# Three layers of scans and attention on one core: softplus's sum on TensorE, late folds for GpSimd's products, and a shorter lag in the last attention

## The chip, the cores and the metric

One core of a Trainium2 chip runs the kernel. The metric is the device time of one execution in microseconds, lower being better; the figure for a kernel is the median of its runs.

## The reference

Four conditioned layers in a row over a batch of B = 2, T = 1024 positions, D = 256 channels, all in float32. Layers 0 and 1 are state-space layers (inner width 512, 16 states per channel; layer 1 has one scan forwards and one backwards), layers 2 and 3 are attention with 16 heads of width 16. Cut to what matters here:

```python
# layer 0; layer 1 does the same twice (z1, and z2 on flipped time)
dt = softplus(dt_r @ dt_proj_w.T + dt_proj_b)          # (b, s, 512)
def step(h, inp):                                      # over s = 1024
    dA = exp(dt_t[:, :, None] * A)                     # A = -exp(A_log)
    h = h * dA + (dt_t * u_t)[:, :, None] * B_t[:, None, :]
    y = einsum('bdn,bn->bd', h, C_t)
y = (ys + u * D_param) * silu(z)

# layer 2: softmax of q over its 16 channels, of masked k over positions
attn = einsum('bhse,bhsd->bhed', k, v)

# layer 3
att = einsum('bnhl,bmhl->bnmh', q, k) + (1 - mask) * -1e6
att = softmax(att, axis=2)
y = einsum('bnmh,bmhl->bnhl', att, v)
h = layer_norm(y) * (1 + scale) + shift
return x + silu(h) @ out_w + out_b
```

## The kernel before

**Scans.** Six scans run one after the other: layer 0 for both batches, then layer 1 forwards and backwards for each batch. A scan has 512 channels x 16 states. A tile is 32 channels x 4 states on the 128 partitions and all 1024 positions on the free axis, so a scan has 64 tiles, and `chain` (L985) goes through them in 192 pairs for all six. One tile needs:

- `decay` (L922): ScalarE makes exp(dt * A) into a PSUM tile `dA` (two of them);
- `inputs` (L928): GpSimd multiplies the spread dt*u with B into an SBUF tile `hb` (eight of them), L930;
- `tile` (L933): VectorE runs the recurrence in one instruction (L941, or L937 backwards), then the product with C is made on VectorE (L944) or, where `far` is set, on GpSimd (L943). `far` is set for the first tile of a pair only, by a counter (`lead`) that adds up how much more VectorE has than GpSimd and takes in the background work that GpSimd was given;
- `fold` (L962): TensorE sums the four states of each channel with a 128x32 matrix into a PSUM bank `ys`, two halves of 512 for each tile. Both tiles of a pair are folded in the next pair, after its first slot of background work.

**Background.** While the scans run, everything else (projections, normalisations, softplus, the attention of the first batch in layer 2, its projections in layer 3) is a queue of Python generators in `Behind` (L798). Twice in each pair `slot` (L832) runs some of their steps: it is given a credit of matmul columns (`RATES`, one for each scan, the credit capped at 2T) and stops where the credit or the budgets for ScalarE and GpSimd are used up. A step ends at a `yield`. `pipe` (L366) starts up to two matmul groups, in two PSUM banks, before it empties the first. The order of instructions on each engine is the order of these calls; nothing reorders it later.

**Softplus** is made in `ssm_inputs` (L550) for each of four blocks of 128 channels: `high` projects dt, `parts` takes |x| and max(x, 0) on ScalarE, ScalarE makes ln(1 + exp(-|x|)), `both` (L602) adds the two on GpSimd (`far_op`, L137, issued at L139) and multiplies with u, also on GpSimd.

**Attention, the tail.** After the last scan the second batch still has layers 2 and 3 to pass, as background work, while `attention` (L1360) already runs layer 3 for the first batch. The heads lie in groups of four; each head has 32 rows of a query and a key tile, of which 16 are the head, one carries a constant and one the row's maximum or the mask. For each of 8 groups (two batches of four) there are 16 steps of maxima (TensorE scores, L1380; VectorE maxima, L1389) and 16 of exponentials (scores again; ScalarE exp; TensorE sums over values, L1420). Maxima run one group, 16 steps, ahead of the exponentials, so the loop has 9 x 16 = 144 steps, the first 16 with maxima alone and the last 16 with exponentials alone. In every step two background slots are run, of one generator step each. PSUM in this stage: six banks `sc` for scores, one `av` for the sums, one `bank` for background work. `layer3` (L1279) projects queries and keys with weights padded to 32 columns a head, so that a group is a full 128 rows.

Of the kernel before, what the change touches and what calls it, by code (L numbers as in the profile page):

```python
# [10 lines left out]
F32 = mybir.dt.float32  # L11
# [19 lines left out]
RATES = (2048, 2048, 1250, 1300, 1500, 1500)  # L31
# [4 lines left out]
for _name, _n in (  # L36
# [6 lines left out]
    ("mask3", 16),  # L43
# [9 lines left out]
def kernel(ctx: ExitStack, tc: tile.TileContext, a: dict, out: bass.AP):  # L53
# [23 lines left out]
    banks = {"bank": 2, "ys": 2, "av": 1, "sc": 6}  # L77
# [106 lines left out]
    def row(name):  # L184

        t = small.tile([P, D], F32, tag="row", name="row", bufs=1)
        nc.sync.dma_start(t, a["rows"][0, ts(_ROWS[name], D)].partition_broadcast(P))
        return t
# [207 lines left out]
    def root(mv):  # L396

        r = small_t((P, mv.shape[1]), "rstd", 4)
        act_f(r, mv[:, :, 1], AF.Ln, bias=eps)
        act_f(r, r, AF.Exp, scale=-0.5)  # L400
        return r

    def refine(mv, r):

        q = small_t((P, mv.shape[1]), "newt", 4)
# [17 lines left out]
    def scaled(src, r, q):  # L423
        o = abuf((P, 4, D))
        for j in range(4):
# [61 lines left out]
    def projected(w, src, func, bias, res, keep=True, to=None, count=None):  # L487
# [18 lines left out]
        def ended(m, ch, ps):  # L506
            take(m, ch, ps)
            held[0] -= 1
            if ch == 1:
                if func is AF.Silu:  # L510
                    yield
# [38 lines left out]
    def ssm_inputs(key, u, w_xp, w_dt, dt_b, st):  # L550
# [58 lines left out]

        two = banks["bank"] == 2  # L610
        pss = [high(0, ch) for ch in range(1 + two)]
        yield
        for d in range(4):
# [9 lines left out]
            if d < 3:  # L623
                pss = [high(d + 1, ch) for ch in range(1 + two)]
            yield
            both(d, dt, dt, dtu, ALU.add)
# [8 lines left out]
    def layer0(b, st):  # L635
# [43 lines left out]
        for m in range(4 if b else 0):  # L679
# [24 lines left out]
            yield  # L704
# [10 lines left out]
    def layer1(b, st1, st2):  # L715
# [16 lines left out]
        def first():  # L732
# [5 lines left out]
            for v in skip:  # L738
                nc.vector.tensor_tensor(v, v, twice(cond["s1"][b], 4), ALU.mult)
                far_op(v, v, twice(cond["o1"][b], 4), ALU.add)  # L740
                yield
# [56 lines left out]
    class Behind:  # L798
# [3 lines left out]
        def __init__(self):  # L802
            self.queue = []
            self.soon = []
            self.credit = 0

# [10 lines left out]
        def step(self):  # L817

            while self.queue or self.soon:
# [5 lines left out]
                try:  # L825
                    least = next(self.queue[0])
                    return max(work[0] - at, least or mode["least"])
# [4 lines left out]
        def slot(self, columns):  # L832
# [7 lines left out]
            self.credit = min(self.credit + columns, 2 * T)  # L840
# [3 lines left out]
            while (self.queue or self.soon) and self.credit > 0:  # L844
# [6 lines left out]
                for key in self.room:  # L851
                    self.room[key] -= spent[key]
                    self.given[key] += spent[key]
                    spent[key] = 0

# [14 lines left out]
    class Scan:  # L870
# [91 lines left out]
        def fold(self, d, cp, k, es):  # L962


            for ch in range(2):
                for j, e in enumerate(es):
# [18 lines left out]
    def chain(scans, rates, early, mid, after):  # L985
# [14 lines left out]
        def fold(p):  # L1000
            i, d, cp, k = pairs[p]
            if k == 0:
                scans[i].begin(d, cp)
            scans[i].fold(d, cp, k, [made["inputs"].pop(2 * p + j) for j in range(2)])
# [24 lines left out]
        lead = 0  # L1029
        for p, (i, d, cp, k) in enumerate(pairs):  # L1030
# [17 lines left out]
            behind.slot(rates[i])  # L1048
            if p:
                fold(p - 1)  # L1050
# [29 lines left out]
            behind.slot(rates[i])  # L1080
            s.tile(4 * d + 2 * cp + 1, k, made["decay"].pop(2 * p + 1), made["inputs"][2 * p + 1])
# [39 lines left out]
    def layer2(b, src, dst):  # L1121
        w_qk, w_vo = [weight("w2", 2, 2 * D, 2 * i * D) for i in range(2)]
        w_k = [w_qk[:, :, D:]]
        mneg_i, mneg = abuf((P, T), I32), abuf()
# [68 lines left out]
        r_bq2 = row("bq2")  # L1193
# [81 lines left out]
        yield from stylize(b, y, "aff2", w_vo[:, :, D:], row("bo2"), src, dst, to=x_of[3][b])  # L1275
# [3 lines left out]
    def layer3(b, st):  # L1279

        xn = []
        w_q, w_k = [[weight("qk_w3", 2, DI, at)] for at in (0, DI)]
# [31 lines left out]

        for g in range(4):
            while b and st["n"] < g:

                yield
            qa, ka = [abuf(pool=act if b else None) for _ in range(2)]

            def put(o, ch, bias, ps):
                act_f(o[:, ts(ch, 512)], ps, AF.Identity, bias=bias)
# [9 lines left out]
            yield  # L1332

# [26 lines left out]
    def attention(sts, done):  # L1360
# [70 lines left out]
        half1 = None  # L1431
        for n in range(-1, len(groups)):
            has_e, has_m = n >= 0, n + 1 < len(groups)
            sts[1]["n"] = n
            half0 = None
            for step in range(2 * NT):
                if half1 is not None:
                    next(half1)
                if step == 9 and has_m:
                    half0 = maxima(n + 1, 0)  # L1440
                if half0 is not None and step < 12:
                    next(half0)
                es = [hb() for _ in range(2)] if has_e else None
                for part in range(2):
                    e = [2 * part, 2 * part + 1]
                    m = [2 - 2 * part, 3 - 2 * part]
                    if not has_m:
                        e, m = (range(4), []) if part == 0 else ([], [])
                    if not has_e:
                        e, m = ([], range(4)) if part == 0 else ([], [])  # L1450
                    made = []
# [239 lines left out]
```

## Time and profile before

| what | value |
|---|---|
| median of three runs | 2152.08 us (2148.35 to 2152.58) |
| the profiled execution | 2153.55 us, span from first to last instruction 2151.8 us |
| TensorE matmul busy | 1702.0 us (79%), granted clock 0.821 on average |
| VectorE busy | 1728.3 us (80%) |
| ScalarE busy | 1165.3 us (54%) |
| GpSimd busy | 1318.0 us (61%) |
| 384 inputs on GpSimd, L930 | 898.5 us, 2368 ns each |
| 384 recurrences on VectorE, L941 and L937 | 877 us, some 2.28 us each |
| 285 products with C on VectorE, L944 | 348.9 us, 1224 ns each |
| 99 products with C on GpSimd, L943 | 234.0 us, 2364 ns each |
| 2048 score records on TensorE, L1380 | 357.8 us |

The times come from a profile of one execution. An engine's busy time is the union of its instructions. A wait is put down to the instruction that released it last. TensorE shows two records for each float32 matmul. The scans run from about 70 to 1475 us, the tail from there to 2152 us.

### The profile page before, as it was taken

Reading aid. Unit: us, or ns where it says so; the run is one execution under the profiler, and the core shown is the slowest. Engines: PE = TensorE matmul, PEld = TensorE weight load, DVE = VectorE, ACT = ScalarE, POOL = GpSimd, SP = SyncE. Lnnn points to the kernel's source line nnn. Section 1 sums busy time; section 2 is a strip of 40 time slices with the busy share of each in tenths; the row PEclk is TensorE's granted clock in tenths of the full one; section 3 lists DMA queues with packets and bytes.
Section 4 is the critical chain, followed back from the end, with each engine's and each line's share of the span. In section 5 each row is a group of like instructions: output and inputs, shape, how many; then the busy total and the mean of one; then the engine's idle time right before and its main releaser. Section 6 shows DMA issues by size and latency. Waiting matters only on the chain.

```text
span 2151.8 us, 22746 instructions
## 1 busy us (share of the span) xinstructions
PE 1702.0 (79%) x8144; PEld 642.7 (30%) x8144; DVE 1728.3 (80%) x1688; ACT 1165.3 (54%) x1631; POOL 1318.0 (61%) x651
## 2 busy tenths in 40 slices
PE   7577876488786747888856778647899999999996
PEld 3132213132231312212313323204344433343333
DVE  4688898898999999999998979996767646777742
ACT  5566675475546446564554445431245555655575
POOL 0799897998899999999997879994001000000000
PEclk9688968598895559959856868856799999999998
DMA  3664367264844545558552253433000100010001
GB/s 110 243 215 134 128 231 257 62 204 157 304 156 148 184 155 176 192 171 293 175 186 101 93 198 107 142 110 118 8 1 23 48 2 2 18 55 1 2 1 37
DMA packets 106117, 265.94 MB, mean 124 GB/s; under 512 B 14123, under 2 KB 38572, under 8 KB 106005
## 3 DMA queue, kind: packets, MB, share of 16 engines
q1 hardware_dynamic: 106004, 264.50, 35.9%
q8 instruction: 64, 1.05, 0.2%
q14 instruction: 49, 0.39, 0.1%
HBM read 196.43 MB, written 67.90 MB: 123 GB/s over the span
## 4 chain that ended last, share of the span: by engine, by line
PE 30%; DVE 14%; POOL 8%; issue 6%; ACT 3%; DMA 1%; SPq 0%; DVEq 0%; ACTq 0%; POOLq 0%
PE sc_t L1380 13%; PE bank_t L93 7%; PE av_t L1420 6%; POOL hb_t L930 5%; DVE dA_t L937 3%; DVE dA_t L941 3%; DVE mh L1389 2%; POOL hb_t L943 2%; ACT act_t L131 2%; PE bank_t L97 1%; PE ys_t L968 1%; DVE hb_t L937 1%; DVE hb_t L944 1%; DVE hb_t L941 1%; ACT dA_t L131 1%
## 5 line engine op out<-in xcount | busy, mean ns | idle before, releaser
L930 POOL TENSOR_TENSOR hb_t<-sp,bc 128x1024 f32<-128x1024 f32 x384 | 898.5, 2368 | 58.1 <-DMA bc<-bc 21.1
L131 ACT ACTIVATE dA_t<-sp,negA 128x1024 f32<-128x1024 f32 x384 | 428.0, 1116 | 526.0 <-DVE hb_t L944 424.4
L968 PE MATMUL ys_t<-hb_t,fold 128*32 128x512 f32 x1536 | 324.6, 799 | 227.2 <-POOL hb_t L943 139.7
L941 DVE TENSOR_TENSOR_SCAN dA_t<-dA_t,hb_t 128x1024 f32<-128x1024 f32 x195 | 445.7, 2286 | 59.6 <-ACT dA_t L131 38.0
L1389 DVE TENSOR_REDUCE mh<-sc_t 128x1 f32<-128x512 f32 x512 | 327.5, 685 | 143.9 <-PE sc_t L1380 143.6
L778 POOL TENSOR_TENSOR act_t<-act_t,row 128x1024 f32<-128x1024 f32 x8 | 18.7, 2350 | 629.2 <-DMA act_t<-x 384.6
L131 ACT ACTIVATE hb_t<-sc_t 128x512 f32<-128x512 f32 x512 | 276.2, 595 | 194.0 <-PE sc_t L1380 193.5
L944 DVE TENSOR_TENSOR hb_t<-dA_t,bc 128x1024 f32<-128x1024 f32 x285 | 348.9, 1224 | 20.9
L1380 PE MATMUL sc_t<-act_t 32*128 32x512 f32 x2048 | 357.8, 660 | 8.6 <-DVE mh L1389 7.4
L943 POOL TENSOR_TENSOR hb_t<-hb_t,bc 128x1024 f32<-128x1024 f32 x99 | 234.0, 2364 | 45.6 <-DVE hb_t L941 39.9
L937 DVE TENSOR_TENSOR_SCAN dA_t<-dA_t,hb_t 128x1024 f32<-128x1024 f32 x90 | 205.6, 2284 | 7.5 <-ACT dA_t L131 4.3
L131 ACT ACTIVATE act_t<-bank_t,cols 128x512 f32<-128x512 f32 (+1 forms) x238 | 151.7, 675 | 89.0 <-PE bank_t L93 73.5
L968 PEld LDWEIGHTS ys_t<-hb_t,fold 128*32 128x32 f32 x1536 | 42.2, 122 | 461.0 <-POOL hb_t L943 193.8
L1420 PE MATMUL av_t<-hb_t,act_t 128*32 128x256 f32 x2048 | 162.5, 391 | 0.4
L1380 PEld LDWEIGHTS sc_t<-act_t 32*128 32x128 f32 x2048 | 124.7, 188 | 125.9 <-issue 72.9
L93 PE MATMUL bank_t<-act_t,w_c_w 128*128 128x512 f32 x256 | 133.1, 671 | 23.6 <-ACT act_t L131 23.6
L941 DVE TENSOR_TENSOR_SCAN hb_t<-dA_t,hb_t 128x1024 f32<-128x1024 f32 x61 | 138.9, 2278 | 0.3 <-ACT dA_t L131 0.3
L139 POOL TENSOR_TENSOR act_t<-act_t 128x1024 f32<-128x1024 f32 x50 | 118.0, 2359 | 2.2 <-ACT act_t L131 1.9
L93 PE MATMUL bank_t<-act_t,w_dt_w 64*128 64x512 f32 x96 | 79.3, 967 | 31.3 <-ACT act_t L131 29.8
L1420 PEld LDWEIGHTS av_t<-hb_t,act_t 128*32 128x32 f32 x2048 | 42.4, 108 | 186.1 <-issue 174.5
L97 PE MATMUL bank_t<-ident,act_t 128*128 128x128 f32 x264 | 61.1, 370 | 42.7 <-ACT act_t L131 40.6
L937 DVE TENSOR_TENSOR_SCAN hb_t<-dA_t,hb_t 128x1024 f32<-128x1024 f32 x38 | 86.6, 2280 | 2.4 <-ACT dA_t L131 2.4
(154 smaller groups left out, 1710.4 us busy)
## 6 DMA issues: line engine op xcount, KB each, us to landing
sp<-dt SPq DMA_DIRECT2D x192, 512.0 KB, 5.7
dt<-act_t SPq DMA_DIRECT2D x48, 512.0 KB, 5.2
bc<-bc SPq DMA_DIRECT2D x48, 512.0 KB, 6.5
u<-act_t SPq DMA_DIRECT2D x24, 512.0 KB, 5.0
fu<-u SPq DMA_DIRECT2D x24, 512.0 KB, 4.0
y<-y SPq DMA_DIRECT2D x96, 128.0 KB, 5.0
g<-act_t SPq DMA_DIRECT2D x16, 512.0 KB, 5.2
fg<-g SPq DMA_DIRECT2D x64, 128.0 KB, 4.2
```

The lines of the kernel that those rows point to most:

```text
L93: nc.tensor.matmul(o, w, x, **kw)
L131: nc.scalar.activation(o, x, func, **kw)
L139: nc.gpsimd.tensor_tensor(o, x, y, op)
L930: nc.gpsimd.tensor_tensor(e, self.sp[c, 1], self.bc[0][k], ALU.mult)
L937: nc.vector.tensor_tensor_scan(h[:, ::-1], dA[:, ::-1], e[:, ::-1], 0.0, ALU.mult, ALU.add)
L941: nc.vector.tensor_tensor_scan(h, dA, e, 0.0, ALU.mult, ALU.add)
L943: return lambda: nc.gpsimd.tensor_tensor(e, h, self.bc[1][k], ALU.mult)
L944: nc.vector.tensor_tensor(e, h, self.bc[1][k], ALU.mult)
L968: nc.tensor.matmul(self.ys[d, cp][at : at + DS, :], fold, e[:, ts(ch, 512)], start=False, stop=(k == NK - 1),)
L1380: nc.tensor.matmul(ps, w[r, ts(at, P)], x[r, ts(wide_at, 512)], start=True, stop=True)
L1389: nc.vector.tensor_reduce(mh[n][:, t, ch, j : j + 1], ps, AX.X, ALU.max)
L1420: nc.tensor.matmul(sums.av[32 * j : 32 * j + 32, ts(part, 256)], sts[b]["v"][t // 2][:, t % 2, 4 * g + j, :], es[j // 2][:, at : at + 256] ...
```

## The change

It has parts in both stages.

In the scans: softplus's sum is made by TensorE (two matmuls with the identity add |.| part and max part into a bank) and copied back by ScalarE, in place of GpSimd's add; the next block's projection is started after it. Where a pair's first product was made on GpSimd, only the second tile is folded at the usual place and the first one after the second slot of the pair. The first two scans give more columns to a slot, the credit's cap is 3T, and a step that yields `ALONE` ends its slot (before each Silu and in layer 1's first normalisation). Layer 2's two bias rows are loaded earlier, with two buffers.

In the tail: the lag between maxima and exponentials is 12 steps (`LAG`), in one loop over 140 steps. Scores and background work share seven `sc` banks. For the second batch, queries and keys are projected unpadded, two blocks of 128 channels, and spread to groups: a memset and an add of the constant rows on GpSimd, then four DMAs a tile. Normalised tiles are scaled on VectorE.

```diff
-RATES = (2048, 2048, 1250, 1300, 1500, 1500)
+ALONE = -1
+RATES = (2600, 2600, 1250, 1300, 1500, 1500)
+LAG = 12
...
-    banks = {"bank": 2, "ys": 2, "av": 1, "sc": 6}
+    banks = {"bank": 2, "ys": 2, "av": 1, "sc": 7}
...
     def scaled(src, r, q):
         o = abuf((P, 4, D))
-        for j in range(4):
+        for j in range(4 if mode["tail"] else 0):
+            nc.vector.tensor_scalar(
+                o[:, j, :], src[:, j, :], r[:, j : j + 1], q[:, j : j + 1], ALU.mult, ALU.add
+            )
+        for j in range(0 if mode["tail"] else 4):
             act_f(
...
+        def summed(x, y):
+            def add(ch):
+                ps = bank()
+                for i, t in enumerate((x, y)):
+                    mm(ps, ident, t[:, ts(ch, 512)], start=(i == 0), stop=(i == 1))
+                return ps
+            yield from pipe(*(
+                (lambda ch=ch: add(ch), lambda ps, ch=ch: act_copy(x[:, ts(ch, 512)], ps))
+                for ch in range(2)
+            ))
...
-            if d < 3:
+            if d < 3 and not (mode["scans"] and two):
                 pss = [high(d + 1, ch) for ch in range(1 + two)]
             yield
-            both(d, dt, dt, dtu, ALU.add)
+            if mode["scans"] and two:
+                yield from summed(dt, dtu)
+                pss = [high(d + 1, ch) for ch in range(2)] if d < 3 else []
+            else:
+                both(d, dt, dt, dtu, ALU.add)
...
-            self.credit = min(self.credit + columns, 2 * T)
+            self.credit = min(self.credit + columns, 3 * T)
...
+                if self.alone:
+                    break
...
             behind.slot(rates[i])
+            split = far
             if p:
-                fold(p - 1)
+                fold(p - 1, (1,) if split else (0, 1))
...
             behind.slot(rates[i])
+            if split:
+                fold(p - 1, (0,))
...
     def layer2(b, src, dst):
+        r_bq2 = row("bq2")
...
-        r_bq2 = row("bq2")
+        r_bo2 = row("bo2")
...
+    def spread_heads(xn, w_qk, mrow, st, put):
+        for c in range(2):
+            flat = []
+            for i, bias in enumerate(("bq3d", "bk3d")):
+                o = abuf()
+                flat.append(o)
+                w = [w_qk[:, :, ts(i, D)]]
+                yield from pipe(*(
+                    (lambda ch=ch: project(w, xn, c, ch),
+                     lambda ps, ch=ch: put(o, ch, col(bias, c), ps)) for ch in range(2)
+                ))
+            for g in (2 * c, 2 * c + 1):
+                while st["n"] < g:
+                    yield
+                both = [abuf(pool=act) for _ in range(2)]
+                for i, t in enumerate(both):
+                    nc.gpsimd.memset(t, 0.0)
+                    nc.gpsimd.tensor_scalar(t, t, col("ones3", i), None, ALU.add)
+                    for j in range(4):
+                        at = 64 * (g % 2) + DH * j
+                        nc.sync.dma_start(t[32 * j : 32 * j + DH, :], flat[i][at : at + DH, :])
+                nc.sync.dma_start(both[1][DH + 1 :: 32, :], mrow)
+                st["qk"].append(both)
+                yield
...
-        for n in range(-1, len(groups)):
-            has_e, has_m = n >= 0, n + 1 < len(groups)
+        going = []
+        steps = 2 * NT * len(groups)
+        for at in range(steps + LAG):
+            has_e, has_m = at >= LAG, at < steps
+            n, step = divmod(at - LAG, 2 * NT)
+            n1, step1 = divmod(at, 2 * NT)
             sts[1]["n"] = n
+            if at % NT == 1 and 0 < at // NT <= 2 * len(groups):
+                going.append(maxima(*divmod(at // NT - 1, 2)))
+            going = [v for v in going if next(v, 0) is None]
...
-    banks["bank"] = 1
-    mode.update(scans=False, tail=True)
+    mode.update(scans=False, tail=True, bank="sc")
```

## The prediction

> **What bounds the kernel now.** I read the tenths first, to find the stages, then the busy time of each stage, then in each stage the waits of the engine that is full.
>
> ```profile
> PE   7577876488786747888856778647899999999996
> DVE  4688898898999999999998979996767646777742
> POOL 0799897998899999999997879994001000000000
> PEclk9688968598895559959856868856799999999998
> ```
>
> Each digit is a slice of 54 us. Up to slice 27 VectorE (DVE) and GpSimd (POOL) are both near full and TensorE (PE) is not: the scans. From slice 28 on GpSimd is empty and TensorE is full at full clock: the last attention. Cut at the turns, the columns being us and then busy us (and instructions) of PE, PEld, DVE, ACT, POOL, the granted clock, the DMA share and GB/s:
>
> ```profile
> 92.00:1474.00 1382.00, 1006.01 (x3270) 351.89 (x3270) 1262.97 (x870) 755.04 (x908) 1267.41 (x610) 0.75 0.50 171
> 1474.00:1560.00 86.00, 74.24 (x260) 39.51 (x255) 55.58 (x104) 14.51 (x25) 5.11 (x3) 0.74 0.18 60
> 1560.00:2105.00 545.00, 536.79 (x4288) 210.93 (x4290) 353.77 (x625) 318.65 (x584) 15.96 (x13) 1.00 0.05 15
> ```
>
> The scans last 1382 us with 1263 on VectorE and 1267 on GpSimd: two bounds of one size, 8% from full. The attention is TensorE's: 537 of 545 us. What the engines wait for within the scans (us in total, times, longest):
>
> ```profile
> PE ys_t L968 <- POOL hb_t L943: 139.7, 36, 8.1
> ...
> ACT act_t L131 <- PE bank_t L93: 55.1, 40, 3.9
> ...
> DVE dA_t L941 <- ACT dA_t L131: 38.0, 22, 4.4
> ...
> DVE act_t L785 <- PE bank_t L93: 19.5, 8, 6.0
> ...
> DVE qmx L1205 <- PE bank_t L93: 8.2, 1, 8.2
> ```
>
> A scan waits for its decay (ScalarE) because ScalarE, in order, sits at an eviction whose matmul stands on TensorE behind a fold that waits for GpSimd's product with C. So a late GpSimd product can reach VectorE over two other engines. Last, one step of the attention without background work:
>
> ```profile
> 2010.47 1.14 PE L1380 MATMUL sc_t<-act_t 32*128 32x512 f32 x8
> 2011.54 0.16 PEld L1420 LDWEIGHTS av_t<-hb_t,act_t 128*32 128x32 f32 x8 [0.76 <-issue]
> 2011.55 0.64 PE L1420 MATMUL av_t<-hb_t,act_t 128*32 128x256 f32 x8
> 2011.63 1.08 ACT L131 ACTIVATE hb_t<-sc_t 128x512 f32<-128x512 f32 x2 [0.78 <-PE sc_t L1380]
> 2011.67 1.29 DVE L1389 TENSOR_REDUCE mh<-sc_t 128x1 f32<-128x512 f32 x2 [0.64 <-PE sc_t L1380]
> ...
> 2012.12 1.43 PE L1380 MATMUL sc_t<-act_t 32*128 32x512 f32 x8
> ...
> 2014.04 1.14 PE L1380 MATMUL sc_t<-act_t 32*128 32x512 f32 x8
> ```
>
> A step is 2014.04 - 2010.47 = 3.57 us, in halves of 1.65 and 1.92. The second set of four scores is the longer by 0.29: with six banks its third and fourth score need the banks of the first set's first two, which ScalarE and VectorE have in hand until 2012.2 and 2012.3.
>
> **The scans, part by part.** (a) 23 softplus sums leave GpSimd (its list of 128x1024 adds falls from 50 to 27): 23 x 2.356 us (median of L139) = 54 us. The counter in the chain spends that: the list has 114 products with C on GpSimd in place of 99, 15 x 2.364 = 35 us back. GpSimd is 19 us lighter, and VectorE by 15 x 1.224 (L944) = 18 us. Since both are full, the stage falls by the same: -18.
>
> [...]
>
> (b) The sums now cost TensorE 23 x 4 matmuls of 128x512, 184 records. Weight loads of a 128x512 stream follow each other by 0.43 us at full clock (638.09, 638.51, 638.94) and by 0.86 in the slow stretch before it (635.16, 636.02, 636.87): 79 to 158 us, under TensorE's 376 idle. ScalarE gets 46 copies of 0.58 us, 27 us, under its 627 idle. The cover matters: a copy stands in ScalarE's queue ahead of a decay. A decay has about 2.2 us to spare (424 us of idle in 196 waits for VectorE to free its tile), so 0.58 fits and a wait for TensorE may not. Bounds: nothing, and 23 x 4.4 us (the longest decay wait) = +102. The stage now has some 200 evictions by ScalarE (222 rows with a column operand, less the tail's) and 45 us of VectorE waiting for decays, 0.22 us each; 46 more are +10, which I take, since each copy is planned a step behind its matmuls.
>
> (c) The fold of a product that GpSimd made comes half a pair later, the other one at once. TensorE's 139.7 us of waiting shrinks; what that gives VectorE lies between nothing and all of its waits for decays and for L785 (45 + 20 = -64). The tile is held half a pair longer, seven of eight in use, so GpSimd's inputs wait no more than now (19 us). I take half of the L785 waits: -10.
>
> (d) The bias row of layer 2 is loaded at the layer's start, not at its use: the chain of waits has that DMA with 4.2 us, VectorE's wait there is 8.2. -4, between 0 and -8. (e) More background per slot in the first two scans, and slots that end before a Silu, move work between slots and take none away: 0, within 10 either way. ScalarE's table pair (1.28 + 1.28 around a Silu of 1.06) then no longer shares a slot with an eviction. Sum: -18 + 10 - 10 - 4 = **-22**.
>
> **The attention.** (f) Queries and keys of the second batch are projected at their true width: 16 matmuls in place of 32. Where one group's 8 matmuls fall into a 20 us window they are 7.94 us of TensorE, 0.99 each, with TensorE busy 20.0 of 20: 16 x 0.99 = -16. In their place come 32 DMAs of 64 KB on SP (some 0.5 us of issue each, on a queue that is idle there) and 8 memsets (0.95) and 8 adds on GpSimd (between 0.95 and the 2.36 of two inputs, at most 27 us on an engine with 16 busy of 545). They are planned done by step 64 of 140, as now; a first group later than that would stop the maxima.
>
> (g) The scores share seven banks with the background work, which had its own. Without background the second set waits for one bank in place of two: between 0 and 0.29 us a step. With a background bank in the rotation it is six again. Of 112 full steps at least 40 have no background and many more have it in one half: 60 x 0.2 = -12, between 0 and 112 x 0.29 = -32.
>
> (h) The exponentials follow the maxima by 12 steps, not 16: 140 steps in place of 144. Four steps of maxima alone (four reductions, 2.47 us) and four of exponentials alone (2.2 us, 2087.14 to 2089.31) become four full ones: 4 x (2.47 + 2.2 - 3.57) = -4, and -15 if the first are counted at their present 5.1 us (81 us for 16). I take -5. (i) 40 normalisations of 128x256 go from ScalarE (0.52) to VectorE (at most 0.48, L1179): neither is full there; 0. Sum: -16 - 12 - 5 = **-33**.
>
> **The sum.** 2151.8 - 22 - 33 = 2097 for the span. The profiled execution took 2153.55, 1.5 over the median of the runs, and its span lies 1.75 inside it, so the median's figure is the same: **2097**.
>
> **Rivals.** First: the scans give back what they gain, because VectorE's wait moves from GpSimd to ScalarE. For it: TensorE is already busy or waiting through the scans, and its clock there is 0.75. Against it: both engines that bound the stage lose 18 us of work. Only the tail counts: 2152 - 33 = 2119, or 2131 without (g).
>
> The Trainium skill, "TensorE: Matmul & The Clock Gate", section "What's actually happening", has a half-rate clock unless TensorE was busy for about 3.4 us on end. The rows agree in kind (0.75 over the scans, 1.00 when TensorE is full). By the rule the sums run at the slow price where TensorE waits between folds, which favours this rival.
>
> Second: more than the sum, because the chain GpSimd, TensorE, ScalarE, VectorE breaks up (half of the 64 in (c)) and (g) reaches its end: 2097 - 22 - 20 = 2055. Against it: half of VectorE's 29 decay waits are under 1.3 us, and those at 207 and 242 us stand behind a table pair, not behind a fold.
>
> Third, slower: the identity sums stop ScalarE. TensorE does an add's matmuls late, behind a fold; the copy waits, the decay behind it waits, VectorE stands. All other terms are -65, so it decides from 65 / 23 = 2.8 us of VectorE per sum; at 4.4 us the time is 2152 - 65 + 102 = 2189. For it: 505 to 510 us, where two evictions waited 1.7 and 3.9 us and the scan behind them 4.4. Against it: those waits are what (c) thins out.
>
> **Chances.** Forecast (2078 to 2112) 0.48; first rival (2112 up to no change) 0.26, of which 0.04 lies within 0.2% of before (4.3 us, what this measurement can tell from nothing); second 0.16; third 0.10. The range leaves out the third, those 0.04 and 0.06 of the second: 2056 to 2144. Faster 0.86, same 0.04, slower 0.10.
>
> **What would show it.** In the profile after: GpSimd about 19 and VectorE about 18 us lighter in the scans, and that stage near 1360 us; the wait of folds for L943's product well below 140 us; ScalarE's waits for evictions not above some 70; a full step of 3.3 to 3.4 us, both sets of scores alike; layer 3's projections 16 us shorter; the stage after the scans near 645 us. Wrong would be decay waits of VectorE over 80 us (third rival), a step still of 3.57, or a stop in the maxima at step 64.

## The result, and the profile after

The changed kernel takes 2176.2 us (median of four runs, 2173.8 to 2180.6), the one before 2152.3 in the same batch: a ratio of 1.0106, 95% interval 1.0069 to 1.0144. It is slower by about 24 us, where 55 us of gain were forecast. The profiled execution took 2177.14 us, its span 2175.1.

The tenths of the page after, 54 us a slice, show the same two stages; the scans now reach into slice 28:

```profile
PE   7466877569897765887886576795899999999997
DVE  4566778898679999999988999899777766777763
POOL 0677777898689999999998887999300310100000
PEclk9687987669998766998998688896789999999998
```

In the five slices from 54 to 326 us VectorE is at 5 to 7, where it was at 6 to 9, and GpSimd at 6 to 7, where it was at 7 to 9. The loss is at the beginning. Cut at the turns (columns as in the prediction: us, then busy us and instructions of PE, PEld, DVE, ACT, POOL, clock, DMA share, GB/s):

```profile
92.00:1537.00 1445.00, 1077.21 (x3453) 377.32 (x3452) 1258.13 (x857) 782.09 (x959) 1268.33 (x602) 0.83 0.47 163
1537.00:1620.00 83.00, 76.05 (x359) 38.64 (x360) 59.84 (x111) 18.00 (x32) 9.80 (x5) 0.81 0.23 77
1620.00:2128.00 508.00, 497.32 (x4132) 191.37 (x4132) 360.64 (x646) 293.60 (x534) 41.47 (x27) 0.99 0.07 17
```

The scans' stage is 1445 us where it was 1382. VectorE has 5 us less to do in it and stands idle 187 us where it stood 119. The attention is 508 us where it was 545. Timed by VectorE's recurrences in the timeline (64 to a scan), in us:

| | first two scans (layer 0) | other four (layer 1) | last recurrence to the end |
|---|---|---|---|
| before | 238.7 + 251.6 = 490.3 | 909.0 | 682.0 |
| after | 294.4 + 269.4 = 563.8 | 899.2 | 641.5 |

So layer 0 lost 73.5 us, layer 1 gained 10 and the tail 40.5, together the 23.3 by which the spans differ. What the engines wait for from 92 to 1537 us (total, times, longest):

```profile
PE ys_t L998 <- DVE hb_t L974: 130.5, 40, 16.1
PE ys_t L998 <- POOL hb_t L973: 37.7, 16, 5.3
...
ACT act_t L135 <- PE bank_t L97: 94.5, 53, 3.9
ACT act_t L139 <- PE bank_t L97: 81.0, 43, 3.9
...
DVE dA_t L971 <- ACT dA_t L135: 81.9, 40, 5.7
DVE hb_t L971 <- ACT dA_t L135: 31.9, 14, 8.1
DVE act_t L811 <- PE bank_t L97: 12.8, 7, 4.3
...
POOL act_t L143 <- ACT act_t L139: 34.2, 10, 6.0
```

The lines to set beside the prediction's: the fold (L998) waits 38 us for GpSimd in place of 140, as the late fold meant it to, but 131 us for VectorE's product, where it waited 86. ScalarE waits 175 us for TensorE where one line of 55 was shown, 81 of it at copies (L139), most of which are the sums' own. VectorE waits 82 us for decays in the first of its lines, where it waited 38. And GpSimd now waits for a copy, which it never did before.

One full step of the last attention:

```profile
2010.29 1.29 PE L1445 MATMUL sc_t<-act_t 32*128 32x512 f32 x8
...
2012.08 1.20 PE L1445 MATMUL sc_t<-act_t 32*128 32x512 f32 x8
...
2013.78 1.29 PE L1445 MATMUL sc_t<-act_t 32*128 32x512 f32 x8
```

It is 3.49 us (3.57 before) in halves of 1.79 and 1.70 (1.65 and 1.92).

What one softplus sum looks like, from the timeline of the first scan (start, duration, engine; in brackets the idle time before, and what ended it):

```profile
73.66 1.15 ACT L135 ACTIVATE act_t<-act_t,one 128x1024 f32<-128x1024 f32 x1
74.71 1.10 ACT L135 ACTIVATE dA_t<-sp,negA 128x1024 f32<-128x1024 f32 x1
74.86 6.64 PE L97 MATMUL bank_t<-act_t,ident 128*128 128x512 f32 x8 [20.40 <-ACT act_t L135]
...
78.73 0.59 ACT L139 COPY act_t<-bank_t 128x512 f32<-128x512 f32 x1 [2.92 <-PE bank_t L97]
...
81.54 0.58 ACT L139 COPY act_t<-bank_t 128x512 f32<-128x512 f32 x1 [2.22 <-PE bank_t L97]
...
82.59 2.42 ACT L135 ACTIVATE act_t<-bank_t,cols 128x512 f32<-128x512 f32 x4 [0.47 <-PE bank_t L97]
...
84.89 1.14 ACT L135 ACTIVATE dA_t<-sp,negA 128x1024 f32<-128x1024 f32 x1
...
86.12 2.30 DVE L971 TENSOR_TENSOR_SCAN dA_t<-dA_t,hb_t 128x1024 f32<-128x1024 f32 x1 [3.76 <-ACT dA_t L135]
```

ScalarE makes Ln; TensorE, in order, has stood for that Ln for 20 us; ScalarE does one decay and then stands 2.92 and 2.22 us in front of the two copies; the next block's four evictions follow; only then comes the next decay, 9.1 us after the one before (75.81 to 84.89), and VectorE has waited 3.76 us for it. The 20 us are the longest such wait; all 184 records together waited 106 us for ScalarE.

### The profile page after: what moved, and what is told of

It is laid out like the page before. It is cut to its first block, busy times and chain, and to the rows that moved or that the text cites. A ratio compares the mean times of both kernels' runs of the same rounds, so it can differ in the third digit from the quotient of the medians.

```text
span 2175.1 us, 23175 instructions
## 1 busy us (share of the span) xinstructions
PE 1735.6 (80%) x8296; PEld 650.2 (30%) x8296; DVE 1735.5 (80%) x1713; ACT 1164.5 (54%) x1629; POOL 1348.3 (62%) x659
## 4 chain that ended last, share of the span: by engine, by line
PE 29%; DVE 11%; POOL 10%; issue 5%; ACT 4%; DMA 1%; SPq 0%; DVEq 0%; ACTq 0%; POOLq 0%
PE sc_t L1445 13%; POOL hb_t L960 6%; PE av_t L1485 6%; PE sc_t L97 4%; PE bank_t L97 3%; DVE dA_t L967 3%; POOL hb_t L973 2%; DVE dA_t L971 2%; ACT act_t L135 2%; DVE mh L1454 2%; PE sc_t L101 2%; PE ys_t L998 1%; DVE hb_t L974 1%; DVE hb_t L967 1%; ACT dA_t L135 1%
## 5 line engine op out<-in xcount | busy, mean ns | idle before, releaser
L960 POOL TENSOR_TENSOR hb_t<-sp,bc 128x1024 f32<-128x1024 f32 x384 | 918.8, 2431 | 83.6 <-PE ys_t L998 52.7
L971 DVE TENSOR_TENSOR_SCAN dA_t<-dA_t,hb_t 128x1024 f32<-128x1024 f32 x185 | 423.0, 2287 | 104.2 <-ACT dA_t L135 85.6
L998 PE MATMUL ys_t<-hb_t,fold 128*32 128x512 f32 x1536 | 351.9, 709 | 168.5 <-DVE hb_t L974 130.5
L974 DVE TENSOR_TENSOR hb_t<-dA_t,bc 128x1024 f32<-128x1024 f32 x270 | 330.7, 1225 | 20.2 <-DVE dA_t L971 0.9
L1445 PE MATMUL sc_t<-act_t 32*128 32x512 f32 x2048 | 336.6, 653 | 10.7 <-DVE mh L1454 7.2
L973 POOL TENSOR_TENSOR hb_t<-hb_t,bc 128x1024 f32<-128x1024 f32 x114 | 272.3, 2388 | 43.3 <-DVE hb_t L971 32.0
L97 PE MATMUL bank_t<-act_t,ident 128*128 128x512 f32 x184 | 128.3, 854 | 105.8 <-ACT act_t L135 105.8
L967 DVE TENSOR_TENSOR_SCAN dA_t<-dA_t,hb_t 128x1024 f32<-128x1024 f32 x85 | 194.2, 2284 | 10.5 <-ACT dA_t L135 9.4
L971 DVE TENSOR_TENSOR_SCAN hb_t<-dA_t,hb_t 128x1024 f32<-128x1024 f32 x71 | 161.9, 2281 | 38.7 <-ACT dA_t L135 31.9
L135 ACT ACTIVATE act_t<-bank_t,cols 128x512 f32<-128x512 f32 (+1 forms) x206 | 130.6, 679 | 97.1 <-PE bank_t L97 89.6
L998 PEld LDWEIGHTS ys_t<-hb_t,fold 128*32 128x32 f32 x1536 | 49.1, 116 | 407.0 <-DVE hb_t L974 209.4
L97 PEld LDWEIGHTS bank_t<-act_t,ident 128*128 128x128 f32 x184 | 47.1, 273 | 185.8 <-ACT act_t L135 126.0
L967 DVE TENSOR_TENSOR_SCAN hb_t<-dA_t,hb_t 128x1024 f32<-128x1024 f32 x43 | 98.0, 2279 | 0.0
L139 ACT COPY act_t<-bank_t 128x512 f32<-128x512 f32 (+2 forms) x77 | 42.5, 560 | 86.2 <-PE bank_t L97 86.1
```

Of the source, the lines that this page charges most:

```text
L97: nc.tensor.matmul(o, w, x, **kw)
L135: nc.scalar.activation(o, x, func, **kw)
L960: nc.gpsimd.tensor_tensor(e, self.sp[c, 1], self.bc[0][k], ALU.mult)
L967: nc.vector.tensor_tensor_scan(h[:, ::-1], dA[:, ::-1], e[:, ::-1], 0.0, ALU.mult, ALU.add)
L971: nc.vector.tensor_tensor_scan(h, dA, e, 0.0, ALU.mult, ALU.add)
L973: return lambda: nc.gpsimd.tensor_tensor(e, h, self.bc[1][k], ALU.mult)
```

## Experiments on the scans

All variants keep the changed tail. Ratios are to the kernel before, with the 95% interval; scan lengths are of the one execution that was profiled, which was 8 us above its median for `rates_back`, 6 for `sums_back` and 5 for `act_alone`, so that differences of a few us between single scans say little. "Idle" is VectorE's idle time from 70 us to the last recurrence.

| label | softplus's sum | rates | median us, ratio | layer 0 | layer 1 | idle |
|---|---|---|---|---|---|---|
| (after) | TensorE | fast | 2176.2, 1.0106 | 563.8 | 899.2 | 192.5 |
| sums_back | GpSimd | fast | 2139.0, 0.9927 [0.9903, 0.9951] | 513.6 | 918.4 | 141.2 |
| rates_back | TensorE | old | 2151.6, 0.9992 [0.9964, 1.0020] | 522.2 | 924.6 | 176.4 |
| sums_rates_back | GpSimd | old | 2125.7, 0.9860 [0.9823, 0.9897] | 494.8 | 917.4 | 125.1 |
| tail_split | GpSimd, no lone slots | old | 2117.1, 0.9830 [0.9797, 0.9864] | 491.4 | 911.0 | 117.8 |
| tail_only | GpSimd, of the scans' edits the early bias rows alone | old | 2115.3, 0.9826 [0.9778, 0.9873] | 488.7 | 909.8 | 114.8 |
| no_alone | TensorE, no lone slots | fast | 2174.7, 1.0104 [1.0072, 1.0135] | 550.1 | 911.7 | 186.4 |
| loads_slow | GpSimd, unread work on PE and ACT | old | 2116.1, 0.9825 [0.9770, 0.9880] | 493.9 | 911.5 | 121.7 |
| loads_fast | GpSimd, unread work on PE and ACT | fast | 2171.9, 1.0087 [1.0054, 1.0120] | 523.0 | 934.5 | 167.7 |
| sums_spaced | TensorE, spaced | old | 2157.3, 1.0013 [0.9992, 1.0034] | 518.3 | 924.5 | 180.5 |
| spaced_fast | TensorE, spaced | fast | 2132.4, 0.9903 [0.9873, 0.9932] | 523.7 | 897.4 | 150.0 |

**Undoing the parts.** Theory S put the loss on the sums, theory R on the rates. `sums_back` puts the sum back on GpSimd, `rates_back` puts back the rates and the cap, and `sums_rates_back` does both:

```diff
-RATES = (2600, 2600, 1250, 1300, 1500, 1500)
+RATES = (2048, 2048, 1250, 1300, 1500, 1500)
-            self.credit = min(self.credit + columns, 3 * T)
+            self.credit = min(self.credit + columns, 2 * T)
...
-            if mode["scans"] and two:
-                yield from summed(dt, dtu)
-                pss = [high(d + 1, ch) for ch in range(2)] if d < 3 else []
-            else:
-                both(d, dt, dt, dtu, ALU.add)
+            both(d, dt, dt, dtu, ALU.add)
```

> The changed kernel with softplus's sum back on GpSimd, all else as changed (rates 2600, cap 3T, ALONE, split folds, the new tail). Theory S (the identity sums stop ScalarE and, through it, VectorE; they cost the scans some 60 us): 2105 to 2125 us, VectorE's waits for decays back from 123 to about 45 us, the last scan near 1470 us. Theory R (the higher rate packs the background of the first two scans too densely, the sums are innocent): 2165 to 2180 us, decay waits still over 100 us in the first two scans.

> The changed kernel with the old rates (2048 for the first two scans) and the old credit cap of 2T, the identity sums kept. Theory S: 2165 to 2180 us, nothing gained. Theory R: 2110 to 2130 us.

> Both of these taken back; left are split folds, ALONE, the early bias rows and the new tail. Theory S: the same as sums_back within 10 us (2105 to 2125). Theory R: the same as rates_back. If both have a part, it is faster than either alone.

> The old order in the scans altogether (sum on GpSimd, old rates, both folds together, no ALONE; only the bias rows of layer 2 stay early), and the new tail. The tail after the last scan took 641 us in the changed kernel against 682 us before, so 2152 - 40 - up to 8 for the rows: 2104 to 2114 us, whatever spoiled the scans. If split folds and ALONE help the scans, sums_rates_back is below this one; the prediction's term for the folds says by 10 us.

Each theory has a part of the loss and neither has all of it: the sums cost 26 us at the old rates and 37 at the fast rates, the rates 13 without the sums and 25 with them. VectorE's idle time in the profiled executions adds up: 16 more by the rates alone, 51 by the sums alone, 67 by both; the medians do not quite: 13 and 26 alone, 51 by both. The sums do take work off VectorE (15 products, its busy time falls by 17 us from `sums_rates_back` to `rates_back`); three times that comes back as idle time. `tail_only`, with the split folds and lone slots gone too, has the lowest median of the study; two of the variants below, `tail_split` (2117.1) and `loads_slow` (2116.1), cannot be told from it.

**The late fold and the lone slots.** `tail_split` is `tail_only` with the late fold; `no_alone` is the changed kernel without the lone slots, those that a step with `ALONE` ends:

```diff
-                if self.alone:
-                    break
```

> tail_only with the late fold of GpSimd's products put in, without ALONE. sums_rates_back, which has both, took 2125.7 us and tail_only 2115.3. If the late fold is what costs the 10 us: 2121 to 2130. If ALONE costs them: 2110 to 2119 (the prediction's term for the fold, a gain of 10, would give 2105). TensorE's wait for GpSimd's product (130 us in tail_only) should fall to some 30 and its wait for VectorE's product rise from 87 to 174, as in sums_rates_back.

> The changed kernel without the slots that end before a Silu and in layer 1's first normalisation. From tail_split against sums_rates_back (2117.1 against 2125.7) the slot ends cost some 8 us: 2168. If they keep ScalarE's queue short and are worth their place when the blocks are long: 2176 to 2190.

What the fold waits for from 92 to 1470 us, in `tail_only` and then in `tail_split`:

```profile
PE ys_t L992 <- POOL hb_t L967: 133.6, 32, 8.5
PE ys_t L992 <- DVE hb_t L968: 82.6, 39, 7.2
```

```profile
PE ys_t L992 <- DVE hb_t L968: 175.2, 63, 9.4
PE ys_t L992 <- POOL hb_t L967: 20.2, 11, 3.8
```

The wait for GpSimd is gone, 113 us of it, and 93 of that stands one instruction on, at VectorE's product of the same pair. The time is the same (2117.1 and 2115.3): the fold was not what the pair waited for. The lone slots seemed to cost 8 us between `tail_split` and `sums_rates_back`; in the changed kernel they cost nothing that can be told (2174.7 against 2176.2).

**Load or order.** The two halves of the sum's work were put in without their use: `pe_alone` has the identity products on u, read by nobody, `act_alone` 46 copies on ScalarE into an unread bank, both with the real sum on GpSimd at the old rates. `loads_slow` has both, with each copy behind its products as in the real sum; `loads_fast` is that at the fast rates.

```diff
             if mode["scans"] and two:
-                yield from summed(dt, dtu)
+                both(d, dt, dt, dtu, ALU.add)
+                yield from summed(u[d], u[d])
...
-   lambda ps, ch=ch: act_copy(x[:, ts(ch, 512)], ps)
+   lambda ps, ch=ch: act_copy(ps, ps)
```

> sums_rates_back (2125.7 us) with the sum on GpSimd, and the identity products issued besides, on a tile long ready (u), to a bank that nobody reads: TensorE's load alone, with no wait for ScalarE's logarithm and no copy. rates_back, which has the sums in full, took 2151.6, so 26 us are to be divided. Theory L (TensorE's load, 23 x 4 matmuls, delays folds and evictions): 2140 to 2152. Theory W (the load fits; the waits of the in-order queues between ScalarE and TensorE cost): 2122 to 2132. It leaves the output as it is.

> sums_rates_back with the sum on GpSimd and two ScalarE copies of 128x512 for each block besides, from a tile long ready into a bank that nobody reads: ScalarE's load alone. Theory W and theory L both: 2122 to 2134 (27 us of copies against 600 us of idle). If ScalarE's own time is what costs (theory A): 2140 to 2152.

> loads_fast with the old rates and the old cap (2048, 2T): unread identity products on u and their copies on ScalarE, each waiting in order for TensorE, the sum itself on GpSimd, split folds and lone slots kept. Reference points: 2125.7 with no such work, 2151.6 with the real sums, 2171.9 for the same work at the fast rates, 2139.0 for the fast rates alone. If ScalarE's in-order wait at each copy is the cost at any rate: 2150 to 2158. If at the old rates only the real chain costs (as the two halves, TensorE alone 2120.6 and ScalarE alone 2123.4, suggest) and the waits bite only where blocks are packed closely: 2120 to 2135.

> The changed kernel with softplus's sum back on GpSimd, but with the identity products on u and their ScalarE copies (from the bank onto itself, read by nobody) left in at the same steps, the fast rates, the split folds and the lone slots kept: TensorE's and ScalarE's extra work and ScalarE's in-order waits for TensorE are there, while no product waits on Ln and no GpSimd product waits on a copy. Theory Q (the work and ScalarE's in-order waits at the fast rates cost the 37 us): 2165 to 2180, the first scan near 290 us. Theory C (the chain Ln, product, copy, product with u costs them): 2135 to 2150, the first scan near 260 us, GpSimd's waits for the copy gone.

At the old rates TensorE's part (2120.6, 0.9839 [0.9810, 0.9867]), ScalarE's (2123.4, 0.9852 [0.9818, 0.9885]) and both together (2116.1) cost nothing against 2125.7. The real sum, with the same instructions, costs 35 us more than both together (2151.6), though it spares GpSimd the adds. So at the old rates the theories of a load on TensorE (L) and on ScalarE (A) fall, unless the steps that the work adds to the plan gave back what the work took (the section on planned steps). The real sum also moves 14 products from VectorE to GpSimd (117 there in `rates_back`, 103 in `loads_slow`), which no run does by itself. The groups of identity products and copies, in `rates_back`:

```profile
L97 PE MATMUL bank_t<-act_t,ident 128*128 128x512 f32 x184 | 131.3, 869 | 112.9 <-ACT act_t L135 112.9
L139 ACT COPY act_t<-bank_t 128x512 f32<-128x512 f32 x58 | 33.3, 583 | 95.9 <-PE bank_t L97 95.9
```

and in `loads_slow`:

```profile
L97 PE MATMUL bank_t<-act_t,ident 128*128 128x512 f32 x184 | 109.0, 733 | 27.0 <-ACT act_t L135 27.0
L139 ACT COPY bank_t<-bank_t 128x512 f32<-128x512 f32 x46 | 24.6, 549 | 6.1 <-PE bank_t L97 6.0
```

(busy us, mean ns, idle us before and what ended it). With a real sum the products wait 113 us for Ln and the copies 96 us for the products; on data that has long been there, 27 and 6. Wait and price go together. The eight records of layer 1's first block, in `rates_back` after 3.78 us of waiting, then in `loads_slow` after 0.50:

```profile
548.97 6.08 PE L97 MATMUL bank_t<-act_t,ident 128*128 128x512 f32 x8 [3.78 <-ACT act_t L135]
```

```profile
530.52 3.70 PE L97 MATMUL bank_t<-act_t,ident 128*128 128x512 f32 x8 [0.50 <-ACT act_t L135]
```

6.08 us against 3.70, and the copies stand in front of it. The granted clock was 1.00 in `rates_back` from 540 to 545 us, 0.75 in the wait from 545 to 549, 0.50 from 549 to 553.4 and 0.88 from there to 555; in `loads_slow` it was 1.00 throughout the set. The weight loads of the slow set follow each other by 0.85 us until 4.4 us after its start, the last by 0.63. The Trainium skill ("TensorE: Matmul & The Clock Gate", section "What you observe") has the change to the faster clock some 4 us into sustained matmuls, give or take half a microsecond. These rows put it between 4.4 and 5.1 us, near that or a little later.

At the fast rates the same unread work costs 33 us (2139.0 to 2171.9), against theory C of that run, although its copies wait only 3.7 us for TensorE; its first scan is 266 us, where theory Q had 290 and theory C 260. It does not lie where the real sums' loss lies: layer 0 is 523.0 us (513.6 without it, 563.8 with the real sums), layer 1 934.5 (918.4 and 899.2). In layer 0, then, the real sum costs 28 us (522.2 against 493.9) and 41 us (563.8 against 523.0) more than its unread copy, at the old and at the fast rates. In layer 1 it costs 13 us more at the old rates and 35 us less at the fast rates, so that over the whole kernel the real sums at the fast rates cost only 4 us more than unread work (2176.2 against 2171.9).

The waits say where layer 0's part arises. In its two scans, in the changed kernel and then in `loads_fast`:

```profile
DVE dA_t L971 <- ACT dA_t L135: 74.9, 33, 5.7
ACT act_t L139 <- PE bank_t L97: 55.1, 27, 3.9
DVE hb_t L971 <- ACT dA_t L135: 25.3, 12, 8.1
```

```profile
DVE dA_t L972 <- ACT dA_t L135: 41.0, 18, 9.5
DVE hb_t L972 <- ACT dA_t L135: 15.9, 7, 6.4
ACT act_t L139 <- PE bank_t L97: 8.7, 5, 2.9
ACT bank_t L139 <- PE bank_t L97: 1.8, 2, 1.1
```

VectorE waits 100 us for decays against 57, a difference of 43 where the two scans differ by 41; at the old rates it is 71 against 49, 22 of the 28. The loss of layer 0 thus reaches VectorE through late decays of ScalarE, while ScalarE's waits in front of copies go from 10 to 55 us.

**Spacing.** Slot ends between Ln, the products and the copies let the scan issue its own decays, inputs and folds in between:

```diff
+            yield ALONE
...
+            made = [add(ch) for ch in range(2)]
+            yield ALONE
+            for ch in range(2):
+                act_copy(x[:, ts(ch, 512)], made[ch])
...
```

> rates_back (2151.6 us; identity sums in full, old rates) with a slot's end put between the logarithm and the identity products, and again between these and their copies, so that neither TensorE nor ScalarE meets work that is not ready. Theory W: 2120 to 2135, with ScalarE's waits for TensorE down from 183 us towards 100. Theory L or A: 2145 to 2157, the load is the same.

> The changed kernel with slot ends between Ln, the identity products and the two copies, so that the scan's own decays, inputs and folds are issued between them, at the fast rates (with the old rates this spacing gave nothing, 2157.3 against 2151.6, and a block then came due late: a stop of 32 us of VectorE at 564 us). If blocks in close packing, three slots' work in one, are what stops the first scan at the fast rates: 2145 to 2162, the first scan below 275 us. If spacing makes the first blocks of the first scan late instead: 2170 to 2190, the first scan 290 us and above.

> spaced_fast with the old rate in the first scan (2048) and the fast one in the second (2600). If the first scan loses by close packing and the second needs the rate to have layer 1's first blocks ready in time: the first scan near 250 us (spaced_fast 270), the second near 255, no stop of VectorE over 15 us near 560 us; 2110 to 2122. If the identity sums keep a cost of their own when they are spaced and in time: 2125 to 2135.

At the old rates spacing gave nothing (2157.3), against theory W as it was put: the blocks then come late, and near the end of layer 0's second scan, where layer 1's first block is due and all that is left of it is issued in one go, VectorE stops 32 us for a decay (564 us); it stops 20.1 there in `rates_back`, 14.6 in `loads_slow`, 9.3 in `sums_rates_back`. At the fast rates, where the blocks are in time, it takes 44 us off (2176.2 to 2132.4): the copies of this shape wait 23.4 us in place of 79.7 and no stop of over 6 us is left there. That is below both expectations, and 7 us below `sums_back`, which has the sum on GpSimd at these rates, but still 17 above `tail_only`. `spaced_mid` (old rate in the first scan only) came to 2134.4, 0.9892 [0.9858, 0.9926], its first scan 262 us where 250 was expected: in it the sums keep a cost even when they are spaced and at the slow rate, VectorE waiting 52 us for decays there (17 in `tail_only`).

**The planned steps alone.** `sums_layer1` has the sums on TensorE in layer 1 only, with the old scan order. (They are 16 of the 23 by the count of products, 128 of 184, not 11.) `tail_steps` is `tail_only` with the four steps and their columns in each block, ahead of the next block's projection, but no work in them.

```diff
             both(d, dt, dt, dtu, ALU.add)
+            yield T
+            yield T
+            yield
+            yield
+            pss = [high(d + 1, ch) for ch in range(2)] if d < 3 else []
```

> The new tail with the old scan order and the old rates, and the identity sums in layer 1's blocks alone (11 of the 23 sums on TensorE and ScalarE, 12 back on GpSimd). Theory P (the sums cost where blocks are due at once: the start of the first scan and the start of layer 1; layer 1's later blocks have slack): 2108 to 2121, within 6 us of 2115.3, the wait of 20 us at the start of layer 1 stays (it is the first block of layer 1, so up to +15 of it may show: then near 2130). Theory E (each sum costs about 1.1 us wherever it stands, 26/23): 2124 to 2132, spread over the scans.

> tail_only (old scans, new tail) in which each softplus block has the four planned steps of the identity sums, with their columns, but none of their work: the next block's projection comes later. loads_slow, which has them, took 2116.1 where the same kernel without them took 2125.7. If the steps themselves place the background better: 2103 to 2110. If they only shift it between scans: 2111 to 2121, with single scans 10 to 25 us longer and shorter than in tail_only.

Both expectations failed. `sums_layer1` took 2143.3 (0.9950 [0.9923, 0.9978]), 28 us above `tail_only`, and `tail_steps` 2136.4 (0.9903 [0.9869, 0.9937]): 21 us for steps in which nothing is done and a projection that comes after them. In both the last scan is the long one, 250.2 and 252.4 us against 212.6, and the third the short one, 216.2 and 214.6 against 232.2. The columns that the steps take from the credit leave more of the other background to the last scan, where VectorE waits 19 us for banks of TensorE (5 in `tail_only`). Yet the same steps with work in them cost nothing in `loads_slow`, which has split folds and lone slots besides. So a lengthened plan is worth between -10 us (with unread work in it) and +21, in no order that these runs explain, and most of what `sums_layer1` lost may be that.

## Experiments on the tail

Each takes one part back, from `tail_only`: `padded` the projections, `six_banks` the ring of seven banks (background in a bank of its own again), `lag16` the lag.

```diff
# padded
-        if mode["tail"]:
-            yield from spread_heads(xn, w_qk, mrow, st, put)
-            return
...
# six_banks
-    banks = {"bank": 2, "ys": 2, "av": 1, "sc": 7}
+    banks = {"bank": 2, "ys": 2, "av": 1, "sc": 6}
...
+        mode["bank"] = "sc"
...
-    mode.update(scans=False, tail=True, bank="sc")
+    banks["bank"] = 1
+    mode.update(scans=False, tail=True)
# lag16
-LAG = 12
+LAG = 16
```

> The new tail and the old scans, with the second batch element's layer-3 projections on padded weights again, as before the change (twice the columns, half the rows at work). The forecast's term (f), 16 us: 2131. If attention's pipeline has room for them beside the steps: 2115 to 2120. If it also stops the steps for the evictions: 2135 and above.

> The new tail and the old scans, with the score ring of six banks and a bank of its own for the rest as before the change (lag 12 and half the projections kept). The forecast's term (g), 12 us: 2127. By the trace of the changed kernel (a step of 3.49 us where it was 3.57, over 64 steps): 2119 to 2122. If the banks are worth nothing: 2115.

> The new tail and the old scans with the exponentials 16 steps behind the maxima, as before the change. Forecast's term (h), 5 us: 2120; at its upper end of 15: 2130; nothing: 2115.

| label | median us, ratio | last recurrence to the end | against 643.3 |
|---|---|---|---|
| padded | 2126.0, 0.9898 [0.9842, 0.9954] | 652.3 | +9 |
| six_banks | 2140.8, 0.9951 [0.9927, 0.9975] | 666.0 | +23 |
| lag16 | 2126.5, 0.9879 [0.9823, 0.9934] | 649.3 | +6 |

The three make 38 us, and the tail went from 682.0 to 643.3: they account for it, and leave nothing that shows for the normalisations on VectorE, which no run takes back by themselves. (By the medians, against 2115.3, they are 11, 26 and 11 us; the runs of `tail_only` alone spread over 11.) The banks are worth the most. From the last recurrence to the first exponential `six_banks` takes 72.9 us and `tail_only` 64.6, so 8.3 us come before the steps begin, in the stage where the background has a single bank; from the first exponential to the last it takes 568 us against 555, 13 us in the steps. ScalarE's exponentials in `tail_only`, then in `six_banks`:

```profile
L135 ACT ACTIVATE hb_t<-sc_t 128x512 f32<-128x512 f32 x512 | 276.7, 595 | 191.1 <-PE sc_t L1439 191.0
```

```profile
L135 ACT ACTIVATE hb_t<-sc_t 128x512 f32<-128x512 f32 x512 | 277.0, 596 | 205.6 <-PE sc_t L1439 205.4
```

The same 277 us of work, and 14 us more of waiting for scores.

## Why the prediction was wrong

The sign was missed in the scans, by terms (b) and (e). Terms (a) and (b), the whole of the moved sum, were forecast at -8 us and measured +26 at the old rates and +37 at the fast rates; (e) was forecast at 0 within 10 and measured +13 and +25. The tail gained 7 us more than was worked out, with its terms off in both directions.

- **(a)** -18: the counter moved 15 products, and VectorE's products fell from 348.9 to 330.7 us, -18.2 as forecast. But it is no gain where VectorE waits: in the first scan it stands idle 86 us (28 in `tail_only`), GpSimd 69 us (17). The step "since both are full, the stage falls by the same" failed; neither was full in the first scan any more. GpSimd, forecast 19 us lighter, has 1268.3 us in the scans where it had 1267.4: its inputs last 2431 ns on average in place of 2368, 20 us in all (918.8 against 898.5), for which no run shows the reason.
- **(b)** +10 was the term that failed. It priced a copy as an average eviction, 0.22 us, "since each copy is planned a step behind its matmuls". A step in the plan is no distance on the chip: Ln, products, copies and the product with u are one chain that crosses from ScalarE to TensorE, back, and on to GpSimd, with little of the scan issued between: one decay in the example above. In layer 0's two scans the changed kernel has 11 of the 23 sums (88 of 184 records); their real use costs 41 us beyond unread work, 3.7 us a sum, and at the old rates 28 us for some 10, 2.7. That is the third rival's place and price, which would decide from 2.8 us a sum if it were paid on all 23; it shows in layer 0 above all, and 2189 was too much. The sign that was named for that rival, decay waits over 80 us, came: 113.8 us in the two lines of L971 above. Its argument against itself, that the late fold thins these waits out, was wrong: the products in front of a copy waited 106 us for ScalarE's Ln, not for a fold.
- **(c)** -10: nothing, or a loss of 2 us within the noise. The fold's wait moved to VectorE's product.
- **(d)** -4: the early bias rows are in `tail_only`, whose last recurrence starts 2.7 us earlier than before (1467.2 and 1469.9 us), but 1.8 of this lie ahead of the first recurrence (68.7 and 70.5). VectorE's wait of 8.2 us is gone (0.8 in `tail_only`), and the two layers' scans together are 1 us shorter, which is within the noise.
- **(e)** 0 within 10: the fast rates alone cost 13 us (`sums_back` against `sums_rates_back`; the first scan is 21.9 us longer), and 25 with the sums. The lone slots cost nothing that can be told. It was priced as if moved work were free. In the first scan of `sums_back` VectorE waits 29 us for decays and GpSimd's inputs 26 us for folds, where `sums_rates_back` has 21 and 8; that a block's instructions stand more closely in the queues in front of them is the likely reason, and not shown.
- **(f)** -16: 9 to 11 us. **(h)** -5: 6 us in the tail. **(g)** -12: 13 us in the steps, and 8.3 before them that the sum did not have. The step of 3.49 us, where 3.3 to 3.4 was named, is one of 116 full steps and does not carry that sum. With -33 forecast, the tail gained 40.5; that the forecast came so near is in part luck, (f) being 5 to 7 us too high and (g) 9 too low.

The first rival, "the scans give back what they gain because VectorE's wait moves from GpSimd to ScalarE", named the right waits and stopped at zero: the 18 us of products that VectorE lost were given back four times over (72 us of idle time, 120.7 to 192.5).

Not settled: why unread work costs 33 us at the fast rates and nothing at the old, why layer 1 is shorter with the real sums at the fast rates than with unread work, and what share of the changed kernel's loss is the placement of the other background, or of the products that went to GpSimd with the sum, rather than the chain. What the runs pin down is the price of the two edits, and that layer 0's excess over unread work reaches VectorE as waits for decays.

## What to carry to other kernels

The busy time of work moved from a full engine to idle ones cost nothing here at the old rates, and its crossings between engines did cost: count how often the new chain enters an in-order queue behind its own producer, and what stands behind it there. Put work of the main loop between the crossings, and look whether the longer chain still meets its due time; here spacing at the old rate gave nothing, the rate without spacing lost 25 us more, and spacing at the fast rate took 44 us off the changed kernel, though not enough to beat leaving the sum on GpSimd at the old rates. And when a plan of background work is changed, time a variant with the steps and no work in them before anything is explained by the work.

## What was not expected of the hardware

The clock that TensorE was granted fell to half within a wait of 3.78 us (1.00 before it, 0.50 after it, in the rows of `rates_back` above), in a stage in which it was busy 76% of the time, and so the price of an instruction went with how late its input was. Over all 184 records the mean was 844 to 869 ns in the three kernels in which they waited over 100 us for Ln (after, rates_back, sums_spaced) and 715 to 761 in the four where they waited 18 to 59 (loads_fast, loads_slow, spaced_fast, spaced_mid). A wait of ScalarE for TensorE was thus longer just where TensorE had first waited for ScalarE.
